# Seven-product block multiplication in the first batch, the factor sum and the gate rows on GpSimd: an AdaLN transformer block on one core

## The chip, the cores and the metric

The kernel runs on one core of a Trainium2 chip. The metric is the device time of one execution in microseconds, the median of several runs. The core has five engines that run side by side and meet through semaphores: TensorE (PE, matrix products into PSUM), VectorE (DVE), ScalarE (ACT), GpSimd (POOL) and SyncE (SP, which here only issues transfers). SP, ACT and POOL each have a queue of their own for DMAs. Each engine runs its instructions in the order that was fixed when the kernel was built. A waiting instruction holds up all that stand behind it.

## What is computed

Four batches of 1024 tokens with 512 channels, all in float32. Each batch is normalised, scaled and shifted by rows that come from a condition vector, goes through attention, is normalised again and goes through a sum of eight 512 x 512 factors.

```python
x = L0_attn_hidden_states                                   # (4, 1024, 512)
mod = (_silu(L0_c) @ L0_wmod).reshape(4, 6, 1, -1)
sa, ca, ga, sb, cb, gb = (mod[:, k] for k in range(6))
ga = (2 * (ga >= 0) - 1) * jnp.maximum(jnp.abs(ga), 0.25)   # gb alike
h = _layernorm(x) * (1 + ca) + sa
qf, kf = h @ Wq.T, h @ Wk.T                                 # rank 64, the same for all 16 heads
attn = softmax(qf @ kf.T)
x = x + ga * ((attn @ (h @ Wv.T)) @ Wo.T)
h = _layernorm(x) * (1 + cb) + sb
x = x + gb * (jnp.einsum('btd,rde->bte', h, factors) / math.sqrt(8) + bias)
```

All heads have the same scores, so one attention matrix per batch is enough, and Wv and Wo are folded into one 512 x 512 matrix (`wvo`). With n the normalised input, the kernel computes Z = attn @ n and then Z @ (scaled wvo). The shift `sa` gives one row per batch, `c1`, which is added to x.

## The kernel before

**One batch.** Tokens are kept as eight tiles of 128. `ln1` (L395) normalises a half of the batch (four tiles) with a reciprocal root on GpSimd (`rstd_of`, L343, the tiles `r_a` and `r_f`) and VectorE passes. The half is transposed: in batch 0 on TensorE, later by VectorE in blocks of 32 x 32 and sixteen 64 KB moves from SBUF to SBUF (`hT_by_dma` L428, `move_blocks` L416; staging tiles `st`, two buffers). `project` (L458) makes queries and keys, `scores` (L505) makes two token tiles of scores and their exponentials, and `transpose_probs` (L540) brings these into `PT`, again by sixteen moves on SP. `scale_wqk` (L450) scales the query and key weights for one batch.

**Z.** For each half of the queries Z is a product over 1024 keys. Batch 0 uses `z_steps` (L572): eight steps, each with four matmuls 512 columns wide, and a ScalarE copy out of PSUM after every second step. Batches 1 to 3 use `z_steps_by_seven` (L636). It cuts both operands in 2 x 2 quarters and needs seven products of quarters (m1 to m7, eight matmuls 256 wide each) where eight would be usual. The sums of quarters that this takes are made by `n_sums` (L612, four GpSimd passes over 128 x 1024, once per batch, three of them into staging tiles and one in place), by `p_sums` (L630, two VectorE passes per half, one of them into the tile `t`), by two more VectorE passes inside m1 and m5, and by adds of the products on VectorE and, in m7, GpSimd.

**Rows.** `shift_rows` (L298) adds up `c1`, `gates` (L308) makes the gate rows `ga`, `gb` and the gated bias on VectorE, four partitions high and 512 wide. `publish` writes a row to DRAM, and `spread` (L239) reads it back into all 128 partitions. The tile `rows` has the buffer in which later the scaled matrices `w` (`make_w`, L696) and `f` (`make_f`, L705) lie.

**The factor sum.** `sum_factors` (L325) runs on GpSimd after the first half of batch 0: sixteen loads of two 128 x 512 pieces into four staging buffers, and 28 adds of 128 x 512 into `fsum`.

**The second part.** `attn_out` (L716) multiplies Z by `w` and adds to x, `ln2` (L734) normalises and transposes by moves (into `st` tiles), `ffn` (L771) multiplies by `f` and stores. The FFN of a batch runs among the Z steps of the next batch's first half.

**Order.** The main loop (L819 to L902) is written out by hand: for each batch the steps of the first half with other work between them, then the steps of the second half with the projections and scores of the next batch between them (`todo`, at the `places`), then `n_sums`, `attn_out`, `ln2`. A scheduler orders each engine's instructions, close to program order; `tc.keep_in_program_order` pins an instruction. PSUM for products has four buffers (`ps_m`) and for scores two (`ps_s`).

Of the kernel before, what the change touches and what calls it, by code (L numbers as in the profile page):

```python
# [30 lines left out]
def kernel(  # L31
# [123 lines left out]
    rows = wbp.tile([32 + B, 4, D], F32, tag="w", name="rows")  # L155
    rows_a, rows_b = rows[0:B], rows[32 : 32 + B]
    biasb = rows_a[:, 3, :]
    nc.sync.dma_start(out=biasb, in_=bias.to_broadcast([B, D]))
    load_xa(1, 0)

# [61 lines left out]
    def gate(g, dst, name):  # L222

        sg = bcp.tile([32 + B, D], F32, tag="bc", name=f"gsign_{name}")[32 : 32 + B]
        ab = bcp.tile([32 + B, D], F32, tag="bc", name=f"gabs_{name}")[32 : 32 + B]
        nc.vector.tensor_scalar(sg, g, 0.0, 2.0, ALU.is_ge, ALU.mult)
        nc.vector.scalar_tensor_tensor(ab, g, -1.0, g, ALU.mult, ALU.max)
        nc.vector.tensor_scalar(ab, ab, 0.25, None, ALU.max)
        nc.vector.scalar_tensor_tensor(dst, sg, -1.0, ab, ALU.add, ALU.mult)
# [9 lines left out]
    def spread(name, b):  # L239
        tl = bcp.tile([P, D], F32, tag="bc", name=f"bc_{name}_{b}")  # L240

        queue = nc.gpsimd if name == "gb" or b == 0 else nc.sync
        queue.dma_start(out=tl, in_=rows_d[name][b : b + 1, :].to_broadcast([P, D]))
        return tl
# [53 lines left out]
    def shift_rows(ps):  # L298
        c1 = rows_a[:, 2, :]
        nc.scalar.copy(c1, ps[:B, :])  # L300
        for kc in range(1, KC):
            nc.vector.tensor_tensor(c1, ps[32 * kc : 32 * kc + B, :], c1, ALU.add)
# [5 lines left out]
    def gates():  # L308
        ga, gb, c1 = rows_a[:, 0, :], rows_a[:, 1, :], rows_a[:, 2, :]
        gate(rows_b[:, 0, :], ga, "ga")  # L310
        publish(ga, "ga")
        nc.vector.tensor_tensor(c1, c1, ga, ALU.mult)
        publish(c1, "c1")
        gate(rows_b[:, 3, :], gb, "gb")
        nc.vector.tensor_tensor(biasb, biasb, gb, ALU.mult)
        publish(biasb, "gbias")
        nc.vector.tensor_scalar(gb, gb, 1.0 / math.sqrt(NR), None, ALU.mult)
        publish(gb, "gb")

    fsum = const.tile([P, KC, D], F32, name="fsum")  # L320
# [4 lines left out]
    def sum_factors():  # L325
        for kc in range(KC):
            for r in range(0, NR, 2):
                f = stage(f"factor_{kc}_{r}").rearrange("p (r d) -> p r d", r=2)
                if kc == 0:

                    nc.scalar.copy(f[0:1, 0, 0:1], ZT[0, 0][0:1, 2, 0:1])
                nc.gpsimd.dma_start(
                    out=f, in_=factors[r : r + 2, ts(kc, P), :].rearrange("r p d -> p r d")
                )
                acc = fsum[:, kc, :]
                if r == 0:
                    nc.gpsimd.tensor_tensor(acc, f[:, 0], f[:, 1], ALU.add)
                else:
                    for k in range(2):
                        nc.gpsimd.tensor_tensor(acc, acc, f[:, k], ALU.add)  # L340
# [65 lines left out]
    bc_c1 = {}  # L406
# [21 lines left out]
    def hT_by_dma(b, g):  # L428
# [9 lines left out]
        move_blocks(st, hT.rearrange("p r k w -> p r (k w)"))  # L438
# [11 lines left out]
    def scale_wqk(b):  # L450
        w = qkp.tile([P, KC, 2 * R], F32, tag="wqkb", name=f"wqk_{b}")
        for kc in range(KC):
            nc.vector.tensor_scalar(
                w[:, kc, :], wqk[:, kc, :], first["ca1"][:, kc, b : b + 1], None, ALU.mult
            )
        wqkb[b] = w
# [83 lines left out]
    def transpose_probs(b, p):  # L540
# [6 lines left out]
            pt_tile(b, half)[:, pair].rearrange("p r j w -> p r (j w)"),  # L547
# [18 lines left out]
    def softmax(b, p):  # L566
        scores(b, p)
        transpose_probs(b, p)

    ZT = {}  # L570

    def z_steps(b, half):  # L572

        zt = ztp.tile([P, KC, GW], F32, tag="zt", name=f"zt_{b}_{half}")
        ZT[b, half] = zt
        hold, steps = {}, []

        def part(dc, jh):
            if jh == 0:
                hold[dc] = psum_mm(f"ps_z_{b}_{half}_{dc}")  # L580
            for j in halves(jh):
                nc.tensor.matmul(  # L582
                    hold[dc], xn1[b, jh][:, j - jh * GT, ts(dc, P)], PT[b, half][:, :, :, j, :],
                    start=(j == 0), stop=(j == NT - 1),
                )
            if jh == 1:
                dst, src = zt[:, dc, :], hold[dc]
                if by_dma(b, half):

                    dst = dst.rearrange("p (h t r a) -> p h r t a", h=2, t=2, r=NQ)  # L590
                    src = src.rearrange("p (h r t a) -> p h r t a", h=2, t=2, r=NQ)
                nc.scalar.copy(dst, src)

        for dc in range(KC):
            for jh in range(2):
                steps.append(lambda dc=dc, jh=jh: part(dc, jh))
        return steps
# [14 lines left out]
    def n_sums(b):  # L612
# [7 lines left out]
        tt(s1, a21, a22, ALU.add)  # L620
# [15 lines left out]
    def z_steps_by_seven(b, half):  # L636
# [8 lines left out]
        def product(k, a, m):  # L645
            ps = psum_mm(f"ps_z_{b}_{half}_m{k}")
            for dc in range(2):
                for j in range(GT):

                    nc.tensor.matmul(  # L650
                        ps[:, ts(dc, 2 * P)], a[:, j, ts(dc, P)],
                        m[:, :, j].rearrange("p r (k a) -> p k r a", k=2),
# [287 lines left out]
```

## Time and profile before

| what | value |
|---|---|
| runs | 541.03, 540.96, 538.78 us; median 540.96 |
| the profiled execution | 538.85 us |
| its span | 537.0 us, granted clock 0.996 |
| TensorE / VectorE / ScalarE / GpSimd busy in the span | 523.4 / 362.1 / 93.2 / 158.5 us |
| first step of Z, batch 0 | 56.84 us |
| first product of Z, batch 1 | 161.29 us |
| GpSimd: factor sum with the sums for batch 1, first to last pass | 87.96 to 145.6 us |
| `fsum` add, 128 x 512, GpSimd | 1.27 us each |
| `n_sums` pass, 128 x 1024, GpSimd | 2.35 us each, 3.38 for two of the first ones |
| `p_sums` pass, 128 x 1024, VectorE | 1.22 us each |
| a 512 KB factor load, issue to landing | 3.7 / 5.1 / 10.2 us (least, median, most) |
| a 64 KB block move on SP, issue to landing | 2.0 us median |

The page counts an engine as busy from the start to the end of its instructions; matmuls overlap, so that the distance between the starts of two groups says better what a group costs. Lines of the timeline give start, length, engine, line of the kernel, operation, output and inputs, shapes and count; what stands in brackets behind them is the idle time before the instruction and what ended it. Lines of the chain give start, length, engine, tile, line.

### The profile page before, as it was taken

What the parts mean: (1) busy time and instruction counts of PE and PEld (TensorE: products, weight loads), DVE (VectorE), ACT (ScalarE), POOL (GpSimd) and SP (SyncE); (2) the same over time, 40 slices, a digit from 0 to 9 for tenths busy, and PEclk for the clock granted to TensorE, in tenths of its full rate; (3) what the DMA queues carried; (4) which work ended last, traced back from release to release, by engine and by line L of the source; (5) the groups of instructions that cost most, each with busy time, mean ns of one, the idle gap of its engine ahead of it and who ended that gap; (6) DMA issues with size and microseconds to landing.
All of it is one profiled execution on the core that took longest, in us unless ns stands there. A gap on an engine that the chain in (4) does not pass through costs nothing.

```text
span 537.0 us, 5254 instructions
## 1 busy us (share of the span) xinstructions
PE 523.4 (97%) x1688; PEld 290.9 (54%) x1688; DVE 362.1 (67%) x580; ACT 93.2 (17%) x155; POOL 158.5 (30%) x177
## 2 busy tenths in 40 slices
PE   6999899999999999999999999999999999999997
PEld 3533344433448457766448457765448457855444
DVE  4629987264899974359999965358999315577761
ACT  1327500122302020123102010123202200000110
POOL 1002136999801353323001343323001134021010
PEclk9989999999999999999999999999999999999999
DMA  8942369858444667404444656404444415001142
GB/s 319 380 182 68 89 179 262 247 165 244 109 118 113 174 209 226 134 1 97 118 113 113 183 157 209 110 0 99 122 119 107 142 59 214 21 0 32 47 157 78
DMA packets 39570, 74.07 MB, mean 138 GB/s; under 512 B 9988, under 2 KB 10756, under 8 KB 39544
## 3 DMA queue, kind: packets, MB, share of 16 engines
q1 hardware_dynamic: 27368, 41.06, 26.8%
q0 software_dynamic: 8624, 28.48, 17.0%
q10 hardware_dynamic: 3552, 4.21, 2.9%
q8 instruction: 13, 0.21, 0.2%
q14 instruction: 13, 0.11, 0.1%
HBM read 35.93 MB, written 8.42 MB: 83 GB/s over the span
## 4 chain that ended last, share of the span: by engine, by line
PE 58%; DVE 20%; issue 8%; SPq 5%; DMA 4%; POOL 3%; ACT 2%; DVEq 0%; POOLq 0%; ACTq 0%
PE ps_z_m L650 17%; PE ps_f L779 15%; PE ps_z L582 8%; PE ps_qk L469 5%; PE ps_o L720 5%; SPq L426 5%; PE ps_wvo L186 3%; DVE pr L544 3%; DVE nm L531 2%; DMA pt<-pr 2%; PE ps_sc L515 2%; ACT pr L535 2%; DVE hT_f L365 2%; DVE x L725 1%; DVE bn_a L356 1%
## 5 line engine op out<-in xcount | busy, mean ns | idle before, releaser
L779 PE MATMUL ps_f<-f,hT_f 128*128 128x512 f32 (+1 forms) x264 | 111.8, 580 | 0.8 <-ACT hT_f L765 0.5
L720 PE MATMUL ps_o<-w,zt 128*128 128x512 f32 x256 | 111.8, 594 | 0.5 <-DVE zt L688 0.5
L779 PEld LDWEIGHTS ps_f<-f,hT_f 128*128 128x128 f32 x264 | 49.9, 190 | 59.4 <-issue 54.3
L720 PEld LDWEIGHTS ps_o<-w,zt 128*128 128x128 f32 x256 | 48.3, 190 | 61.2 <-issue 56.4
L650 PE MATMUL ps_z_m<-pt,xn_a 128*128 128x256 f32 x288 | 65.3, 380 | 0.0
L650 PEld LDWEIGHTS ps_z_m<-pt,xn_a 128*128 128x128 f32 x288 | 54.6, 190 | 11.4 <-issue 2.4
L582 PE MATMUL ps_z<-pt,xn_a 128*128 128x512 f32 x128 | 56.9, 597 | 0.0
L784 DVE TENSOR_TENSOR x<-ps_f,x 128x512 f32<-128x512 f32 (+1 forms) x33 | 21.9, 670 | 43.8 <-PE ps_f L779 43.8
L535 ACT ACTIVATE pr<-ps_sc,nm 128x1024 f32<-128x1024 f32 x32 | 35.5, 1111 | 79.1 <-DVE nm L531 40.9
L650 PE MATMUL ps_z_m<-pt,s 128*128 128x256 f32 x192 | 43.6, 380 | 0.0
L650 PEld LDWEIGHTS ps_z_m<-pt,s 128*128 128x128 f32 x192 | 36.3, 190 | 8.5 <-issue 3.9
L582 PEld LDWEIGHTS ps_z<-pt,xn_a 128*128 128x128 f32 x128 | 23.8, 190 | 31.6 <-issue 30.8
L515 PE MATMUL ps_sc<-kT,qT 64*128 64x512 f32 x128 | 38.2, 626 | 2.3 <-ACT pr L535 2.3
L531 DVE TENSOR_REDUCE nm<-ps_sc 128x1 f32<-128x1024 f32 x32 | 37.6, 1210 | 2.4 <-PE ps_sc L515 2.4
L765 ACT ACTIVATE hT_f<-st_f,mod_sb,mod_cb 128x512 f32<-128x512 f32 x28 | 20.6, 803 | 96.6 <-DVE bn_f L356 40.2
L351 POOL TENSOR_TENSOR r_f<-v_f,mhalf 128x4 f32<-128x4 f32 x8 | 9.3, 1165 | 94.8 <-DVE v_f L347 94.8
L725 DVE SCALAR_TENSOR_TENSOR x<-ps_o,ri,x 128x512 f32<-128x512 f32 x32 | 23.8, 743 | 15.1 <-PE ps_o L720 15.0
L544 DVE STREAM_TRANSPOSE pr<-pr 128x2048 f32<-128x2048 f32 x14 | 32.2, 2299 | 0.9 <-DMA pt<-pr 0.7
L351 POOL TENSOR_TENSOR r_a<-v_a,mhalf 128x4 f32<-128x4 f32 x8 | 9.2, 1152 | 78.8 <-DVE v_a L347 78.6
L340 POOL TENSOR_TENSOR fsum<-fsum,factor 128x512 f32<-128x512 f32 x24 | 30.4, 1273 | 0.4
L469 PE MATMUL ps_qk<-hT_a,wqk 128*128 128x512 f32 x64 | 30.5, 624 | 0.0
L483 DVE TENSOR_SCALAR qT<-ps_qk,qbias 64x512 f32<-64x512 f32 x8 | 5.9, 743 | 36.1 <-PE ps_qk L469 36.1
(124 smaller groups left out, 582.7 us busy)
## 6 DMA issues: line engine op xcount, KB each, us to landing
pt<-pr SPq DMA_DIRECT2D x224, 64.0 KB, 2.0
factor<-in_factors_dram POOLq DMA_DIRECT2D x16, 512.0 KB, 5.1
hT_a<-st_a SPq DMA_DIRECT2D x96, 64.0 KB, 4.9
out_dram<-x POOLq DMA_DIRECT2D x24, 256.0 KB, 2.6
x<-in_x_dram POOLq DMA_DIRECT2D x24, 256.0 KB, 5.3
xa<-in_x_dram POOLq DMA_DIRECT2D x20, 256.0 KB, 4.0
st_f<-hT_f SPq DMA_DIRECT2D x62, 64.0 KB, 2.0
st_f<-hT_f ACTq DMA_DIRECT2D x60, 64.0 KB, 2.1
```

The source lines that it names most:

```text
L340: nc.gpsimd.tensor_tensor(acc, acc, f[:, k], ALU.add)
L426: queues[i % len(queues)].dma_start(out=dst[ts(c, Q), r], in_=src[ts(r, Q), c])
L469: nc.tensor.matmul(ps[: 2 * R, :], wqkb[b][:, kc, :], hT[:, kc] if b == 0 else hT[:, :, kc], start=(kc == 0), stop=(kc == KC - 1),)
L515: nc.tensor.matmul(ps[:, ts(h, 512)], qT[h * R : (h + 1) * R, ts(i, P)], kT[h * R : (h + 1) * R, :], start=True, stop=True,)
L531: nc.vector.tensor_reduce(nm, ps, AX.X, ALU.max, negate=True)
L535: nc.scalar.activation(pr, ps, AF.Exp, bias=nm, scale=1.0, accum_out=den[:, k : k + 1])
L544: nc.vector.transpose(pr2, pr2)
L582: nc.tensor.matmul(hold[dc], xn1[b, jh][:, j - jh * GT, ts(dc, P)], PT[b, half][:, :, :, j, :], start=(j == 0), stop=(j == NT - 1),)
L650: nc.tensor.matmul(ps[:, ts(dc, 2 * P)], a[:, j, ts(dc, P)], m[:, :, j].rearrange("p r (k a) -> p k r a", k=2), start=(j == 0), stop=(j == ...
L720: nc.tensor.matmul(ps, ZT[b, half][:, kc, ts(j, P)], wb[b][:, kc, :], start=(kc == 0), stop=(kc == KC - 1),)
L725: nc.vector.scalar_tensor_tensor(xi, ps, rinv[b][:, t : t + 1], xi, ALU.mult, ALU.add)
L779: nc.tensor.matmul(ps, hT2[b, g][:, kc, ts(j, P)], fb[b][:, kc, cols], start=(kc == 0), stop=(kc == KC - 1),)
```

## The change

Four things are changed.

1. Batch 0 uses the seven products too, for both halves; the old `z_steps` is gone and `z_steps_by_seven` takes its name. So `n_sums(0)` and `p_sums(0, ·)` come in, and in batch 0 the two adds of m7 go to VectorE. Places for the next batch's projections and scores in batch 0's second half are steps 1 to 5 instead of 0 and 2 to 5.
2. The factors are summed in passes of 128 x 1024, into `fsum`, which is loaded with factor 0 by SP at the start. Factors 1 to 7 come as 1 MB loads on GpSimd's queue into the two `st` buffers of the block moves. A one-element copy that reads `w_0` stands before the first add, and `sum_factors()` moves into the second half of batch 0, with `n_sums(1)` behind it.
3. The gate rows, the sum of `c1` and the gated bias are made on GpSimd, with scratch rows in spare partitions of the tile `rows`. `gates` is split in `attention_rows` and `ffn_rows`; the first comes earlier, the second later. ScalarE copies three instead of one of the four pieces of `c1`.
4. In batch 0 half of the moves of the last probabilities and of the second half's transposes go to ACT's queue. `add_c1(0)` moves into the second half, and the query and key weights of batches 2 and 3 are scaled at a fixed place.

```diff
-    rows = wbp.tile([32 + B, 4, D], F32, tag="w", name="rows")
+    rows = wbp.tile([64 + B, 4, D], F32, tag="w", name="rows")
+    fsum = const.tile([P, KC, D], F32, name="fsum")
+    nc.sync.dma_start(out=fsum, in_=factors[0].rearrange("(kc p) d -> p kc d", p=P))
...
+    def gate(g, parts, dst):
+        half, size = parts
+        tensor_scalar = nc.gpsimd.tensor_scalar
+        tc.keep_in_program_order(
+            tensor_scalar(half, g, 0.0, 0.5, ALU.is_ge, ALU.subtract)
+        )
+        tensor_scalar(size, g, 1.0, None, ALU.mult)
+        nc.gpsimd.tensor_tensor(size, size, half, ALU.mult)
+        tensor_scalar(size, size, 0.125, 4.0, ALU.max, ALU.mult)
+        nc.gpsimd.tensor_tensor(dst, size, half, ALU.mult)
...
     def shift_rows(ps):
+        for kc in range(KC - 1):
+            nc.scalar.copy(rows_a[:, kc, :], ps[32 * kc : 32 * kc + B, :])
         c1 = rows_a[:, 2, :]
+        nc.vector.tensor_tensor(c1, ps[32 * (KC - 1) : 32 * (KC - 1) + B, :], c1, ALU.add)
...
+    def attention_rows():
+        ga, c1 = rows_a[:, 0, :], rows_a[:, 2, :]
+        for kc in range(2):
+            nc.gpsimd.tensor_tensor(c1, c1, rows_a[:, kc, :], ALU.add)
+        gate(rows_b[:, 0, :], [rows_c[:, k, :] for k in range(2)], ga)
+        publish(ga, "ga")
+        nc.gpsimd.tensor_tensor(c1, c1, ga, ALU.mult)
+        publish(c1, "c1")
+    def ffn_rows():
+        gb = rows_a[:, 1, :]
+        gate(rows_b[:, 3, :], [rows_c[:, k, :] for k in range(2, 4)], gb)
+        nc.gpsimd.tensor_tensor(biasb, biasb, gb, ALU.mult)
+        publish(biasb, "gbias")
+        nc.gpsimd.tensor_scalar(gb, gb, 1.0 / math.sqrt(NR), None, ALU.mult)
+        publish(gb, "gb")
...
     def sum_factors():
+        f = {}
+        def load(r):
+            f[r] = stp.tile([P, KC, D], F32, tag="st", name=f"factor_{r}")
+            nc.gpsimd.dma_start(
+                out=f[r], in_=factors[r].rearrange("(kc p) d -> p kc d", p=P)
+            )
+        load(1)
+        load(2)
+        late = small.tile([P, 1], F32, tag="late", bufs=1, name="late")
+        nc.gpsimd.tensor_copy(late[0:1], wb[0][0:1, KC - 1, 0:1])
+        for r in range(1, NR):
+            for k in range(2):
+                part = fsum[:, ts(k, 2), :]
+                add = nc.gpsimd.tensor_tensor(part, part, f[r][:, ts(k, 2), :], ALU.add)
+                tc.keep_in_program_order(add)
+            if r + 2 < NR:
+                load(r + 2)
...
     def n_sums(b):
+        if b == 0:
+            nc.gpsimd.tensor_copy(s1[0:1, 0, 0:1], wqkb[0][0:1, KC - 1, 0:1])
...
+            engine = nc.vector if b == 0 else nc.gpsimd
+            engine.tensor_tensor(c(0, 1), c(0, 1), c(1, 1), ALU.add)
+            engine.tensor_tensor(c(1, 1), c(1, 1), c(1, 0), ALU.add)
...
     scale_wqk(0)
+    n_sums(0)
...
+    p_sums(0, 0)
...
         if b == 0:
+            both = nc.sync, nc.scalar
             z0 = z_steps(b, 0)
             z0[0]()
-            softmax(0, 3)
+            softmax(0, 3, *both)
+            z0[1]()
+            shift_rows(ps_c1)
+            attention_rows()
+            z0[2]()
             ln1(1, 0)
             hTn = [hT_by_dma(1, 0)]
-            shift_rows(ps_c1)
-            for step in z0[1:3]:
+            for step in z0[3:5]:
                 step()
             ln1(1, 1)
-            hTn.append(hT_by_dma(1, 1))
-            gates()
-            scale_wqk(nb)
-            for step in z0[3:5]:
-                step()
-            add_c1(0, range(NT))
+            bc_ga[0], bc_c1[0] = spread("ga", 0), spread("c1", 0)
+            hTn.append(hT_by_dma(1, 1, *both))
             for step in z0[5:]:
                 step()
+            scale_wqk(nb)
             second_channels()
-            sum_factors()
+            ffn_rows()
...
-            places = (0, 2, 3, 4, 5)
+            places = (1 if b == 0 else 0, 2, 3, 4, 5)
...
+            if b == 0 and k == 0:
+                add_c1(b, range(NT))
             if k == 1:
                 make_w(b)
+                if b == 0:
+                    sum_factors()
+                    n_sums(1)
...
         if nb is not None:
-            n_sums(nb)
+            if b > 0:
+                n_sums(nb)
```

## The prediction

> **What bounds the kernel now.** I read the busy table first, then TensorE's timeline, then the chain that ended last, in order of time, and last GpSimd's and VectorE's timelines where the first batch hands over to the second (85 to 185 us).
>
> ```profile
> PE 523.4 (97%) x1688; PEld 290.9 (54%) x1688; DVE 362.1 (67%) x580; ACT 93.2 (17%) x155; POOL 158.5 (30%) x177
> ```
>
> TensorE is nearly always busy, so fewer products should pay, unless something else then ends last. TensorE's timeline gives the prices (start, length, count):
>
> ```profile
> 87.19 7.13 PE L582 MATMUL ps_z<-pt,xn_a 128*128 128x512 f32 x16
> 142.10 1.99 PE L515 MATMUL ps_sc<-kT,qT 64*128 64x512 f32 x8
> 161.29 3.62 PE L650 MATMUL ps_z_m<-pt,xn_a 128*128 128x256 f32 x16
> 164.74 3.62 PE L650 MATMUL ps_z_m<-t,s 128*128 128x256 f32 x16
> ```
>
> From start to start a quarter of an eight-product half costs 6.97 us (94.16 - 87.19) and one of seven products 3.45 us (164.74 - 161.29). The chain in order of time shows what TensorE meets next:
>
> ```profile
> 153.59 1.05 POOL r_f L351
> 154.66 1.92 DVE hT_f L365 x4
> 157.24 2.22 DVE hT_f L755
> ...
> 180.29 1.32 DVE xn_a L365 x3
> 182.26 7.13 PE ps_f L779 x16
> ```
>
> From 143 to 182 us the chain is hardly on TensorE: VectorE works without a pause, and TensorE's third FFN tile (182.26) waits 0.5 us for VectorE to free PSUM. VectorE's list starts after the GpSimd reciprocal root r_f, 27.6 us before (182.26 - 154.66). So a lead that TensorE wins in batch 0 reaches the end only as far as r_f moves. GpSimd ahead of it:
>
> ```profile
> 142.03 2.34 POOL L623 TENSOR_TENSOR s<-xn_a,s 128x1024 f32<-128x1024 f32 x1
> 144.34 1.25 POOL L340 TENSOR_TENSOR fsum<-fsum,factor 128x512 f32<-128x512 f32 x1
> 145.55 0.57 POOL L243 DMA_DIRECT2D bc_gb<-rows_gb  x1
> 153.59 1.04 POOL L351 TENSOR_TENSOR r_f<-v_f,mhalf 128x4 f32<-128x4 f32 x1 [7.48 <-DVE v_f L347]
> ```
>
> GpSimd had 7.5 us to spare. The last view is the contention (groups of instructions, and VectorE's timeline):
>
> ```profile
> L700 DVE SCALAR_TENSOR_TENSOR w<-wvo,mod_ch_a,bc_ga x16: 741/746/2061, 89.0 to 448.5; 128x512 f32<-128x512 f32 x16
> 88.97 7.33 DVE L700 SCALAR_TENSOR_TENSOR w<-wvo,mod_ch_a,bc_ga 128x512 f32<-128x512 f32 x4
> 207.23 2.73 DVE L700 SCALAR_TENSOR_TENSOR w<-wvo,mod_ch_a,bc_ga 128x512 f32<-128x512 f32 x4
> ```
>
> The same four passes take 2.73 us alone and 7.33 us beside GpSimd's sums: each waits for a whole GpSimd instruction. It goes the other way too: GpSimd's s took 3.38 us at 223.92, where a VectorE pass over two SBUF tiles was running, against 2.35 us alone.
>
> **The change, part by part.** *Products.* Sixteen quarter-steps in pairs (eight of 6.97) become 14 products of 3.45: 55.8 - 48.4 = 7.4 us less on TensorE. In the built order the first two score tiles of batch 1 are no longer split by a projection: 4 matmuls took 1.9 us each time (104.56, 112.67), 8 take 1.99 at 142.10; 1.9 us less. TensorE's lead is about 9 us.
>
> *VectorE in batch 0.* Per half it gains four 1024-wide passes (1.2 us, L633, L634, L662, L667), five PSUM adds of 0.69 and two SBUF adds of 0.6, some 9.5 us; it loses the gates (11 passes, 6.5 us) and two row sums (1.4). Its idle time covers that: 5.1 us before 83.98, 11.7 before 110.20, 6.8 before 135.34. Without the cover, an add that frees PSUM would stall the product after next; I allow 0.6 us at m4.
>
> *GpSimd before the products.* The four sums of batch 0 (4 x 2.35) run at 28 to 38 us, where GpSimd waited 30 us for v_a; the key weights of batch 1 (0.86 us at 36.6) may wait for one of them, before 2.4 us of idle. The gate rows run from about 61 to 72 us, in its 13.7 us of idle before 65.5; behind them stand the second root r_a of batch 1 (ready to start at 73), four xa loads and two spreads. Two-input rows I cost as the 512-wide sum, 1.27 us. One-input rows no row shows: between 0.29 (the 128-wide select) and 1.27; I take 0.8, near the nearer width. The FFN rows (some 7 us) end at 86.
>
> A page only: the Trainium skill, GPSIMD Engine Reference, section Engine selection, keeps elementwise work on VectorE and calls GpSimd about half as fast with two inputs and about line rate with one. By that the one-input rows would be 0.5 us, and the rows 1 to 2 us shorter, ahead of a wait anyway.
>
> *Queues.* SP loses 16 of 64 moves (0.65 us each) to ACT, and gets the first factor's 1 MB load, long landed when SP starts moving at 55.4. ACT waits in its queue for the last transposes (about 79.4), ends its moves at 84.7, and its next work, the copy of m1, comes at 87.5. SP is done at about 88 instead of 100.6. The batch 2 and 3 weights are scaled earlier, in VectorE's 1.5 us idle at 199.75.
>
> *The factor sum.* It now starts when w_0 is written. When is that? m1 starts at 56.84 like the old product; 3.45, score halves 1.91, six products 20.7, the allowance 0.6 and transposes 0.6 give the second half at 84.1. Two products and a projection (6.9 + 3.4) reach 94.5; VectorE then has the tail of the t update, qT 0.7 and w 2.73: 98.4. No allowance and no t tail: 97.5; every two-input pass of the first half behind one GpSimd row: 101. GpSimd's queue from there, all in front of r_f:
>
> - 14 sums of 1024 x 2.35 = 32.9 and the four sums of batch 1, 9.4
> - six factor loads issued, at 0.54 for 128 rows of 2 KB (x) and 0.72 for 256 (factor), so an estimated 1.08 for 512: 6.5
> - two spreads 1.1 and a one-element copy 0.1
>
> Together 50.0 us: 148.4 if nothing waits. Then VectorE's two-input passes while it runs (2 x 0.6 for m7, 2 x 1.2 for the p sums): 0 to 3.6 us; I take 3.0, since s took the whole of such a wait. Then landings: a load is wanted 1.08 + 4.7 + 1.08 = 6.9 us after its issue. Two 512 KB loads issued 1.95 us apart (116.67, 118.62) were in after 7.2 us; 1 MB of wmod took 8.5 among other loads. So waits are 0 to 4 us over five loads; I take 1.0. GpSimd is free at 152.4.
>
> The Trainium skill sees a danger there: SBUF — State Buffer, section SBUF: two separate sides, says a VectorE pass in a two-port mode keeps GpSimd from writing the descriptors of its own DMAs. The factor issues here took 704 to 736 ns, the one at 113.50 beside such a pass included, so the row shows none of it; by the page each of the few meetings would add the length of one such pass, 0.27 us (wqk).
>
> *VectorE up to r_f.* Scores 6 and 7 of batch 1, at 142.10 before, come at about 133; v_f was ready 11.4 us later, now up to 3.6 more for the two p sums under GpSimd's lock: 148. So GpSimd, not VectorE, ends last, and r_f starts at 152.4 against 153.59. VectorE's order from there to 182 is the same, and it is full, so everything after moves by **-1.2 us**; later batches are unchanged. Sum: 538.85 (the profiled execution: span 537.0 and 1.85 around it) - 1.2 = 537.7. The three runs (541.03, 540.96, 538.78) average 540.26, 1.4 above the profiled one: **539.1 us**. The cost hidden here is TensorE's lead: it stands idle for about 8 us between 165 and 175.
>
> **Rivals.** *A, the forecast, no change:* GpSimd is free between 150.9 and 156.3, -2.7 to +2.7 us. For it: the work listed is 50 us whatever its order. *B, faster:* sums meet no passes and loads land in time; GpSimd is free at 148.4, r_f waits for v_f at 148 instead, -5.1 us: 535.2. Against it: the 3.38 us of s. Its far end, that VectorE catches up between 155 and 182 and TensorE keeps all 9 us, gives 531; against it, no idle in that list but three waits of 0.9 us on GpSimd. *C, slower:* the factor chain takes the place of TensorE. With w_0 at 101, 50.0 of work, 3.6 of passes and 4 of landings GpSimd is free at 158.6, +5.0: 545.3. It decides from 156.3 on. For it: two buffers where four were, and all of it in front of r_f in one queue. *D, that the products stay eight,* is excluded by the built order (14 groups of eight 256-wide matmuls).
>
> **How the numbers follow.** A measurement of this kernel can't tell less than 0.5%, 2.7 us, from no change (its runs differ by 2.2). A has 0.43, B 0.33 (0.04 of it the far end), C 0.24; these are the chances of same, faster, slower. A alone spans 536.4 to 541.8. The range reaches to B's and C's ends: 535.0 to 545.0.
>
> **What would show it.** Right: products at 3.45 us apart in batch 0; the first of batch 1 near 152 instead of 161.3; GpSimd without a gap from w_0 to r_f; VectorE idle before hT_f for GpSimd; TensorE idle before ps_f. r_f ready well before v_f would be B; long waits of fsum for factor loads, or w_0 after 101, C. Wrong altogether: a stall of TensorE before 130 us (a late t or PSUM), or a late r_a, neither of which I find.

## The result and the profile after

| | before | after |
|---|---|---|
| median of 20 runs each | 540.64 us (538.78 to 541.95) | 542.08 us (540.34 to 544.54) |
| after / before | | 1.0029, interval 1.0017 to 1.0042 |
| profiled execution, span | 538.85 us, 537.0 us | 542.55 us, 540.8 us |
| GpSimd's root r_f starts | 153.59 us | 156.09 us |
| TensorE's first product of batch 1 | 161.29 us | 158.11 us |
| TensorE's first qk of batch 2 | 216.78 us | 220.78 us |

The kernel became 1.4 us slower, 0.29%: less than the 0.5% named as the bound of "no change", but on the other side of zero from the forecast. The profiled execution of before lies 1.8 us below its median, that of after 0.5 us above, so the two traces differ by more (3.8 us of span) than the medians do. The busy table of after:

```profile
PE 518.0 (96%) x1784; PEld 310.5 (57%) x1784; DVE 376.4 (70%) x589; ACT 91.5 (17%) x149; POOL 188.6 (35%) x175
```

TensorE has 5.4 us less to do (523.4 before) and yet the span grew: work was removed from a place that no longer ends last. TensorE's timeline (start, length, engine, line, operation, tiles, count, and in brackets the idle time ahead and who ended it), first in batch 0, then in batch 1:

```profile
66.85 3.62 PE L657 MATMUL ps_z_m<-pt,xn_a 128*128 128x256 f32 x16
70.30 3.62 PE L657 MATMUL ps_z_m<-pt,s 128*128 128x256 f32 x16
...
158.11 3.62 PE L657 MATMUL ps_z_m<-pt,xn_a 128*128 128x256 f32 x16
...
165.01 3.62 PE L657 MATMUL ps_z_m<-pt,xn_a 128*128 128x256 f32 x16
173.62 6.05 PE L657 MATMUL ps_z_m<-pt,s 128*128 128x256 f32 x16 [4.99 <-DVE pt L668]
179.50 13.90 PE L790 MATMUL ps_f<-f,hT_f 128*128 128x512 f32 x32
```

Products in batch 0 stand 3.45 us apart (70.30 - 66.85), as forecast, and TensorE comes to batch 1 3.2 us earlier than before. Then it stands still for 4.99 us before product m6, and the 16 matmuls of m6 take 6.05 us instead of 3.62. The chain of waits in order of time says what m6 waited for:

```profile
156.09 1.06 POOL r_f L373
157.18 1.92 DVE hT_f L387 x4
...
172.34 1.15 DVE pt L668
173.62 6.05 PE ps_z_m L657 x16
```

From r_f to m6 it is VectorE's list again, as before; and r_f itself starts 2.5 us later than before (153.59). GpSimd's timeline shows why (L347 issues the load of a factor):

```profile
75.89 1.07 POOL L373 TENSOR_TENSOR r_a<-v_a,mhalf 128x4 f32<-128x4 f32 x1
...
95.31 0.81 POOL L347 DMA_DIRECT2D factor<-in_factors_dram  x1 [0.62 <-DMA hT_a<-st_a]
...
103.58 0.76 POOL L347 DMA_DIRECT2D factor<-in_factors_dram  x1 [5.04 <-DMA hT_a<-st_a]
...
104.49 4.65 POOL L359 TENSOR_TENSOR fsum<-fsum,factor 128x1024 f32<-128x1024 f32 x2
...
153.65 2.35 POOL L627 TENSOR_TENSOR s<-xn_a,s 128x1024 f32<-128x1024 f32 x1
156.09 1.05 POOL L373 TENSOR_TENSOR r_f<-v_f,mhalf 128x4 f32<-128x4 f32 x1
```

There is no gap ahead of r_f: GpSimd is what ends last. Its sum starts at 104.49, not at the forecast 98.4, and the instruction just ahead of it, the issue of factor 2's load at 103.58, had waited 5.04 us for the moves out of the st buffer that it takes over. VectorE's timeline shows the other thing that the sum waits for, w_0:

```profile
77.00 1.92 DVE L387 TENSOR_SCALAR xn_a<-xa,mv,r_a 128x512 f32<-128x512 f32 x4 [5.37 <-DMA pt<-pr]
...
92.38 5.32 DVE L434 TENSOR_TENSOR x<-x,bc_c 128x512 f32<-128x512 f32 x8
...
99.41 2.73 DVE L708 SCALAR_TENSOR_TENSOR w<-wvo,mod_ch_a,bc_ga 128x512 f32<-128x512 f32 x4
```

VectorE normalizes batch 1's tile at 77.00, right after r_a, which takes 1.07 us from 75.89 on (the bracket names a DMA; the same row in the run p2 below names r_a). From there to the end of w_0 (102.14 = 99.41 + 2.73) no row of VectorE shows idle time. So w_0 was late because VectorE was, and the sum was later still by 2.35 us because of the buffer.

### The profile page after: what moved, and what is told of

Read it like the earlier page. It is cut to its first block, busy times and chain, and to the rows that moved or that the text cites. A ratio compares the mean times of both kernels' runs of the same rounds, so it can differ in the third digit from the quotient of the medians.

```text
span 540.8 us, 5461 instructions
## 1 busy us (share of the span) xinstructions
PE 518.0 (96%) x1784; PEld 310.5 (57%) x1784; DVE 376.4 (70%) x589; ACT 91.5 (17%) x149; POOL 188.6 (35%) x175
## 4 chain that ended last, share of the span: by engine, by line
PE 51%; DVE 22%; issue 9%; DMA 7%; SPq 6%; POOL 2%; ACT 1%; ACTq 1%; DVEq 0%; POOLq 0%
PE ps_z_m L657 18%; PE ps_f L790 17%; SPq L448 6%; PE ps_o L731 5%; PE ps_qk L494 5%; DVE nm L556 3%; PE ps_wvo L188 3%; DMA pt<-pr 3%; DVE pr L569 3%; DMA hT_a<-st_a 2%; DVE hT_f L387 2%; DVE bn_f L378 1%; DVE x L736 1%; ACT pr L560 1%; PE ps_sc L540 1%
## 5 line engine op out<-in xcount | busy, mean ns | idle before, releaser
L657 PE MATMUL ps_z_m<-pt,xn_a 128*128 128x256 f32 x384 | 87.3, 381 | 0.6 <-DVE zt L690 0.6
L657 PEld LDWEIGHTS ps_z_m<-pt,xn_a 128*128 128x128 f32 x384 | 72.6, 190 | 16.3 <-issue 2.6
L657 PE MATMUL ps_z_m<-pt,s 128*128 128x256 f32 x256 | 60.6, 392 | 5.0 <-DVE pt L668 5.0
L657 PEld LDWEIGHTS ps_z_m<-pt,s 128*128 128x128 f32 x256 | 50.0, 197 | 17.2 <-issue 10.5
L540 PE MATMUL ps_sc<-kT,qT 64*128 64x512 f32 x128 | 36.1, 624 | 2.5 <-ACT pr L560 2.5
L666 ACT COPY zt<-ps_z_m 128x512 f32<-128x512 f32 x8 | 4.7, 585 | 176.2 <-PE ps_z_m L657 104.4
L359 POOL TENSOR_TENSOR fsum<-fsum,factor 128x1024 f32<-128x1024 f32 x14 | 32.9, 2368 | 1.8 <-DMA factor<-in_factors_dram 1.6
L798 POOL DMA_DIRECT2D out_dram<-x x24 | 13.2, 549 | 57.8 <-DVE x L795 47.5
L657 PE MATMUL ps_z_m<-t,xn_a 128*128 128x256 f32 x128 | 29.4, 383 | 0.5 <-DVE zt L678 0.5
L657 PE MATMUL ps_z_m<-t,s 128*128 128x256 f32 x128 | 29.0, 380 | 0.0
```

The costliest lines, as they stand in the source:

```text
L359: add = nc.gpsimd.tensor_tensor(part, part, f[r][:, ts(k, 2), :], ALU.add)
L540: nc.tensor.matmul(ps[:, ts(h, 512)], qT[h * R : (h + 1) * R, ts(i, P)], kT[h * R : (h + 1) * R, :], start=True, stop=True,)
L657: nc.tensor.matmul(ps[:, ts(dc, 2 * P)], a[:, j, ts(dc, P)], q, start=(j == 0), stop=(j == GT - 1),)
```

## The experiments

The theory after the result: *the end of the kernel follows r_f, and r_f follows the start of the factor sum*. Rivals: the landings of the factor loads, the SP queue, the halved rate of m6's matmuls, and the products themselves. In the expectations W stands for "VectorE, held up behind r_a, makes w_0 late", H for "TensorE's clock falls in its idle time". Ratios are to before, measured on the same chip beside each kernel, with 95% intervals, and need not equal the quotient of the two medians; after stands at 1.0029. One profiled execution of each was read, and the times of one kernel spread by 2 to 9 us, so a single r_f is good to a us or two, not to tenths.

**Half of the factors (e3).** Does r_f follow the sum at all? Factors 4 to 7 are left out, so the FFN weights lack them.

```diff
-        for r in range(1, NR):
+        for r in range(1, NR // 2):
...
-            if r + 2 < NR:
+            if r + 2 < NR // 2:
```

> Factors 4 to 7 are left out of the sum (the FFN's weights then lack them), so GpSimd has 21 us less ahead of r_f. Theory G (GpSimd's queue sets r_f): r_f starts when v_f is written, and v_f, free of GpSimd's lock, comes at about 151.5 instead of 155.9; -4.5 us at r_f, no idle of TensorE worth naming ahead of the fourth product, no halved clock there, which takes off another 1.4: -5.5 to -6 us (536.5). Rival V (VectorE's added passes in batch 0 and 1 bind): v_f stays at 153.8 or later, -2 us or less.

Measured: 535.45 us (534.4 to 539.4), ratio 0.9907 [0.9884, 0.9930]. GpSimd's and TensorE's timelines:

```profile
150.50 1.05 POOL L373 TENSOR_TENSOR r_f<-v_f,mhalf 128x4 f32<-128x4 f32 x1 [19.20 <-DVE v_f L369]
```

```profile
168.57 3.62 PE L657 MATMUL ps_z_m<-pt,s 128*128 128x256 f32 x16
```

GpSimd now has 19.20 us to spare and r_f waits for VectorE's v_f, 3.1 us earlier than before; m6 has neither the idle time nor the slow matmuls. Removing half of the sum is worth 6.6 us against after (542.08 - 535.45). The chain in front of r_f is what the change lost its gain to.

**One load on another queue (e2).** Factor 2's load, whose wait kept GpSimd from the first add, is put on SP.

```diff
-            nc.gpsimd.dma_start(
+            (nc.sync if r == 2 else nc.gpsimd).dma_start(
```

> The load of factor 2 is issued by SP instead of GpSimd, so that GpSimd doesn't stand behind the buffer that the block moves still read. Theory Q: the sum starts at the landing of factor 1 or at w_0, about 102.7 instead of 104.5, r_f -1.7 us; TensorE idles about 3.3 us ahead of the fourth product of batch 1 instead of 5.0, about as long as the 3.4 us after which the clock fell in the changed kernel: -1.7 us if it still falls, -3.1 if it doesn't. Rival R: the 5 us wait only takes the place of waits for factors that would have come later: within 0.5 us.

Measured: 541.39 us (539.9 to 546.8), ratio 1.0030 [0.9997, 1.0063]. In the trace the sum starts 1.7 us earlier (102.77), right after w_0, and r_f 1.3 us earlier (154.79). In the time that can't be told from after. The 2.35 us of the buffer are real, but they are the smaller part; w_0 is the larger. The clock fell here as well: TensorE stood idle for 4.93 us ahead of m6, whose matmuls took 5.30 us.

**Rows of the gate earlier (e5).** If W holds, GpSimd's order ahead of r_a sets w_0. The first four rows of the attention gate are issued as soon as their input exists; only the last stays where it was, just ahead of the row's way to DRAM.

```diff
-        nc.gpsimd.tensor_tensor(dst, size, half, ALU.mult)
+        return lambda: nc.gpsimd.tensor_tensor(dst, size, half, ALU.mult)
...
-        gate(rows_b[:, 0, :], [rows_c[:, k, :] for k in range(2)], ga)
+        ga_last()
...
+    ga_last = gate(rows_b[:, 0, :], [rows_c[:, k, :] for k in range(2)], rows_a[:, 0, :])
```

> The first gate's rows, all but the last pass, are put on GpSimd as soon as the modulation rows are there (about 54 us), ahead of the shift rows; nothing else is moved. GpSimd was idle from 54.8 to 61.5. Theory W (w_0 hangs on r_a): VectorE runs without a pause from the normalization that waits for r_a (77.0) to the end of w_0 (102.1), and r_a stands behind the rows (75.9, where v_a was ready at 71.6). Then r_a comes at 71.7 to 72.7, w_0 3 to 4 us earlier (98 to 99), the factor sum starts at 100 to 101, r_f moves by -3 to -4 us, time -3 to -4 (-5 if TensorE's idle falls under 3.4 us and its clock holds). Rival P (TensorE's products and their waits set w_0, as the forecast had it): w_0 stays at 101 or later, less than 1 us. Rival K: the rows at 54 to 61 hold up VectorE's two-input passes there by 2 us or more, v_a comes later, and the gain is lost.

Measured: 540.49 us (539.2 to 544.7), ratio 1.0002 [0.9982, 1.0022]. r_a comes 3.8 us earlier (72.09) and w_0 3.1 us earlier (99.06), so W is right. But the st buffer comes free only 1.9 us earlier than in after, and the sum starts at 102.62; GpSimd's timeline:

```profile
101.71 0.76 POOL L347 DMA_DIRECT2D factor<-in_factors_dram  x1 [6.28 <-DMA hT_a<-st_a]
```

So two conditions were late side by side, and curing one leaves the other. In the profiled execution, which took 544.67 us, GpSimd also waited 2.08 and 3.47 us for factor loads.

**Both cures (e8)**, the edits of e5 and e2 together.

> The same early gate rows, and the load of factor 2 issued by SP. Theory W with Q: besides, the sum starts at w_0 or at the landing of factor 1 (98 to 99 us) instead of at the freeing of the buffer; r_f -4.5 to -5.5 us against the changed kernel (151 to 151.5), TensorE's idle ahead of the fourth product 3 us or less, clock not halved: time -5.5 to -7 (535.5 to 536.5). Rival: factor 2's landing only takes over, no more than the early gate alone.

Measured: 542.78 us (537.2 to 546.6), ratio 1.0016 [0.9987, 1.0045], without the longest run. A miss: the sum starts at 100.24, 4.2 us earlier than in after, and GpSimd is done at 150.0, but r_f still starts at 156.15, now waiting 6.12 us for v_f. VectorE's timeline shows a new cost:

```profile
117.53 5.48 DVE L686 TENSOR_TENSOR zt<-zt 128x512 f32<-128x512 f32 x1
...
124.07 4.68 DVE L687 TENSOR_TENSOR zt<-zt 128x512 f32<-128x512 f32 x1
...
130.96 0.65 DVE L690 TENSOR_TENSOR zt<-ps_z_m,zt 128x512 f32<-128x512 f32 x1
```

These two adds, both of whose operands lie in SBUF, now meet the factor sums and take seven to eight times what the add of the same width with a PSUM operand takes (0.65). The prediction had priced them at 0.6 us under VectorE's idle time. A sum that starts earlier can fall on them; in e5 and p2 the second add took 4.48 and 4.36 us, in after the first one 2.13.

**Eight products in batch 0 again (e9)**, with everything else of the change kept; batch 0's part sums go with them.

```diff
-    n_sums(0)
...
-            z0 = z_steps(b, 0)
+            z0 = z_eight(b, 0)
...
-        z1 = z_steps(b, 1)
+        z1 = z_steps(b, 1) if b > 0 else z_eight(b, 1)
```

> Batch 0 with eight products per half as before the change (and without its sums on GpSimd and VectorE); the factor sum, the rows on GpSimd and the queues as in the changed kernel. Theory G: TensorE's shorter batch 0 buys nothing, since r_f waits for GpSimd. TensorE works 7.4 us longer and VectorE some 19 us less before 135 us; w_0 is written at 96 to 99, the sum starts at the freeing of the second half's buffer (101 to 103) instead of 104.5, r_f -1.5 to -3 us; TensorE has no idle time of 3 us ahead of the fourth product of batch 1, and its clock holds there: -3 to -4.5 us against the changed kernel (537.5 to 539). Rival L: the seven products do win their 3 us of lead at the end, and without them the time is 545 or more.

Measured: 545.86 us (544.6 to 547.4), ratio 1.0096 [1.0071, 1.0122]. I had expected it faster; it is slower. VectorE's qT now waits 6.74 us for TensorE's projection, w_0 ends at 104.7 and r_f starts at 156.87. So the seven products do pay: beside the rest of the change they are worth 0.67% (1.0096 - 1.0029), some 3.6 us. The two traces show 2.0 us of it (542.8 - 540.8), 0.8 at r_f, which two earlier conditions, the buffer (104.85) and w_0, hold together here; the rest I can't place. Part of it may be chance: in this execution the granted clock was at 0.50 from 57.8 to 61.2, and the first eight matmuls of Z took 5.40 instead of 3.70 us; in after it was at 0.50 for as long near 30 us. The other parts of the change, without the products, cost about 1% (1.0096).

**TensorE kept busy (e6).** Ten products of 512 columns more, into the PSUM tile that m6 then overwrites, fill the idle time before m6. (The view counts each float32 product twice, ten as x20.)

```diff
+            if (b, half, k) == (1, 0, 6):
+                for _ in range(10):
+                    nc.tensor.matmul(
+                        ps, xn1[1, 1][:, 0, ts(0, P)], xn1[1, 1][:, 1, :], start=True, stop=True
+                    )
```

> Ten extra products of 128x512, whose result is overwritten, fill most of TensorE's 5 us wait ahead of the fourth product of batch 1. Theory H: the clock halves because TensorE stood idle; with the extra products those 16 matmuls take 3.6 us instead of 6.05, and the time falls by up to 1.4 us (VectorE then frees the third FFN tile's place only at r_f + 27.6); the planner also orders a few VectorE passes after them differently, +-1 us. Rival: the clock falls for another reason (what the chip does at that time): the 16 matmuls take 6 us still, time unchanged or later.

Measured: 552.42 us, ratio 1.0213 [1.0173, 1.0252]. TensorE's timeline:

```profile
168.03 8.75 PE L653 MATMUL ps_z_m<-xn_a 128*128 128x512 f32 x20
176.61 3.62 PE L662 MATMUL ps_z_m<-pt,s 128*128 128x256 f32 x16
...
192.92 9.18 PE L795 MATMUL ps_f<-f,hT_f 128*128 128x512 f32 x16 [5.82 <-DVE zt L683]
```

With no idle time ahead, m6's 16 matmuls take 3.62 us: H is right about the 6.05. The time is of no use: the planner, given longer work on TensorE, put transposes ahead of VectorE's zt adds, TensorE then waited 5.82 us, and the 16 matmuls behind that took 9.18 us instead of 7.03. H is seen a second time there.

**Two sums behind the root (e7).** Instead of starting the chain earlier, it is made shorter: the last two part sums of batch 1 go behind r_f.

```diff
-        tt(s2, s1, a11, ALU.subtract)
-        tt(s4, a12, s2, ALU.subtract)
+        def rest():
+            tc.keep_in_program_order(tt(s2, s1, a11, ALU.subtract))
+            tt(s4, a12, s2, ALU.subtract)
+        if b == 1:
+            later.append(rest)
+        else:
+            rest()
...
+            if b == 0:
+                later.pop()()
```

> The last two of the four sums of batch 1 (4.7 us of GpSimd) are put behind r_f instead of ahead of it; the planner then also puts VectorE's two sums of probabilities (t, pt) behind r_f. Theory G: r_f starts when GpSimd is free, near 151.3, or at v_f: -4 to -5 us at r_f; the two sums and VectorE's passes after r_f hold each other up, 1 to 3 us; time -2 to -4. Rival V: VectorE's list from r_f to the third FFN tile only gets longer by what was put into it (t and pt, 2.4 us, and the locks, 3 us): time unchanged or later.

Measured: 537.93 us (535.9 to 541.2), ratio 0.9944 [0.9917, 0.9971]. r_f starts at 151.18, 4.9 us earlier than in after, and waits for v_f; m6's idle time is 0.90 us and its matmuls run at the full rate. The moved sums now lie beside hT_f, whose four passes take 5.97 us instead of 1.92, and the kernel is still 0.56% faster than before. This one edit turns the change from a loss into a gain.

**With the early gate (e11: e5 and e7)**

> The early gate rows and the last two sums of batch 1 behind r_f together. Theory: GpSimd is ready for r_f at 149.5 to 150, but v_f comes at 150.5 to 151, so r_f moves by no more than 0.7 against the two sums alone (537.9): 537.2 to 538. Rival: the earlier sum meets the block moves and VectorE's passes, v_f comes later, 539 or more.

Measured: 537.60 us (535.2 to 539.5), ratio 0.9942 [0.9918, 0.9966]; **and with the load on SP too (e10: e5, e2 and e7)**

> The same with the load of factor 2 on SP. Theory V: GpSimd is ready for r_f at 147 to 148, v_f sets it at 150.5 to 151 or later: VectorE's two adds over zt alone are held up by GpSimd's pairs of sums in some runs (5.5 and 4.7 us in the run of the early gate with this load). 537 where they are not, 540 to 541 where they are: a wide spread. Rival G: every us that GpSimd gains still counts, 535.5.

Measured: 538.53 us (533.9 to 541.0), ratio 0.9954 [0.9925, 0.9982]. Neither differs from e7 beyond its interval: once r_f waits for v_f, an earlier start of GpSimd shows no further gain in the times. (In the one execution of e11 that was traced, its second fastest, r_f does come 3.4 us earlier than in e7's, 147.78, and more than the expected 0.7.)

**The zt adds off VectorE (b5)**: e10, and the adds that e8 showed waiting are given to GpSimd, as in the later batches, for all but the first half of batch 0.

```diff
-            engine = nc.vector if b == 0 else nc.gpsimd
+            engine = nc.vector if (b, half) == (0, 0) else nc.gpsimd
```

> The same, and the two adds over zt after the fifth product of batch 0's second half are put on GpSimd (2.5 us there), as in the later batches, so that VectorE meets no lock there. Theory V: v_f at 150 to 150.5 in all runs, GpSimd ready for r_f at 150: 536 to 537, with less spread than the kernel before it. Rival: GpSimd's queue is longer again and r_f comes at 151.5 or later: 538 or more.

Measured: 536.17 us (535.5 to 537.7), ratio 0.9920 [0.9901, 0.9938], 0.8% faster than before and 1.1% faster than after. Against e10 the spread falls from 7.0 to 2.2 us; the intervals of the two overlap. GpSimd's and TensorE's timelines:

```profile
148.70 1.05 POOL L373 TENSOR_TENSOR r_f<-v_f,mhalf 128x4 f32<-128x4 f32 x1 [1.27 <-DVE v_f L369]
```

```profile
168.59 3.69 PE L662 MATMUL ps_z_m<-pt,s 128*128 128x256 f32 x16 [0.90 <-DVE pt L673]
```

r_f starts 7.4 us earlier than in after (156.09 - 148.70), GpSimd is 1.27 us ahead of VectorE there, and m6 starts 5.0 us earlier, at full rate. The two engines end nearly together there, so that shifting more work from GpSimd to behind r_f should have little left to give; that was not tried.

**The SP queue.** In after SP issues its moves of hT_a from 75.57 on over 22.49 us, and 10.2 us of that is one wait (78.7 to 89.0) for an earlier hT_a move. It must be one of ScalarE's, which were issued from 81.94 on, since no move took over 6.0 us to land. e1 puts all moves of batch 1 back on SP:

```diff
-            hTn.append(hT_by_dma(1, 1, *both))
+            hTn.append(hT_by_dma(1, 1))
```

> All 16 moves of batch 1's second half are issued by SP, as before the change; the 8 of the last transposes of batch 0 stay on ScalarE. Theory Q (queues): SP's 10.2 us pause after its fifth move of the first half comes from lanes that ScalarE's moves of the second half hold. It goes; the two waits of ps_qk (1.0 and 1.7 us) and most of the 5.0 us wait of the second factor load go; the factor sum starts at w_0, near 102 instead of 104.3; r_f moves 156.1 to about 154.0. TensorE's lead grows by up to 2.7, so it idles 5 us or more ahead of the fourth product of batch 1 and its clock still halves there: time about -2 us against the changed kernel (540). Rival R (rows): the gate rows on GpSimd are what is late, SP's pause is covered: within 0.5 us. Rival L: TensorE's lead carries to the end: -4.8 us.

Measured: 548.09 us (547.2 to 549.4), ratio 1.0137 [1.0098, 1.0177], the opposite of what was expected. SP has no pause any more and is done at 95.8 instead of 98.1. But the planner dealt the two st buffers out otherwise: factor 2 got the one that factor 1 holds, its load went out at 107.8 only, behind factor 1's adds, and GpSimd waited 5.88 us for it; r_f starts at 161.75. **e12** gives that load to SP as well (e1 and e2):

> All moves of batch 1's second half on SP alone, and the load of factor 2 issued by SP behind them, so that it can't slip behind the first sums on GpSimd as it did when the moves alone were put on SP (548.1 us). Theory: that kernel was slow because factor 2 was then loaded late (GpSimd waited 5.9 us for it) and the sum met the block moves later on; with the load in place the sum starts at w_0 near 102.4, r_f comes at 154 to 155, and the time is that of the load alone (541.4), 540 to 542: the pause of SP itself costs nothing at the end. Rival: the moves of the second half on SP alone are what costs, or the order that the planner then gives to scores and sums: 546 to 548 again.

Measured: 547.53 us, ratio 1.0114 [1.0084, 1.0144], a miss again, for the same reason. GpSimd's timeline:

```profile
115.27 2.36 POOL L359 TENSOR_TENSOR fsum<-fsum,factor 128x1024 f32<-128x1024 f32 x1 [6.75 <-DMA factor<-in_factors_dram]
```

In **p2** the two buffers get names of their own, so that factor 2 can't be given factor 1's:

```diff
-    stp = ctx.enter_context(tc.tile_pool(name="stp", bufs=2))
+    stp = ctx.enter_context(tc.tile_pool(name="stp", bufs=1))
...
-            f[r] = stp.tile([P, KC, D], F32, tag="st", name=f"factor_{r}")
+            f[r] = stp.tile([P, KC, D], F32, tag=f"st{1 - r % 2}", name=f"factor_{r}")
```

> All moves of batch 1's second half on SP, the load of factor 2 on SP behind them, and the two buffers told apart by name, so that factor 2 gets the second half's buffer and not that of factor 1 (which cost 6.8 us of waiting in the kernel before this one). Theory: SP has no pause, factor 2 is loaded by 97 to 98 us and in by 104; the sum starts at w_0 near 102.5 and meets no wait for factor 2; r_f at 154 to 155 as with the load alone on SP, time 540 to 542. Then the shared lanes cost nothing beyond the late buffer. Rival: moves on SP alone are themselves worse, 546 or more. Second rival: freed of the pause, the projections no longer wait (2.4 us), r_f comes at 152 and the time is 538 or less.

Measured: 540.89 us (539.2 to 544.8), ratio 1.0001 [0.9982, 1.0019]. The load goes out at 96.64, nothing waits for it, the sum starts right after w_0 (102.14) and r_f at 154.48: as e2. So e12 lost its 6 us to the shared buffer, and e1, with the same wait, most likely too; SP's pause of 10.2 us cost nothing that shows beyond the late buffer. **p3** is b5 with SP alone and these buffers:

> The fastest kernel so far (536.2: early gate, load of factor 2 on SP, two sums behind r_f, two zt adds on GpSimd) with the second half's moves on SP alone and the buffers told apart by name. Theory: its r_f waits for v_f, and v_f for the block moves of the probabilities, not for the second half: 535.5 to 537. Rival: the projections' waits (0.4 and 2.3 us there) reach the end: 533.5 to 534.5. Rival: the moves on SP alone cost, 540 or more.

Measured: 536.42 us, ratio 0.9921 [0.9903, 0.9940], the same as b5, with r_f at 148.69. Which queue moves the blocks doesn't matter for the end here.

The same relation runs through all of them (spans and starts of r_f in us):

| kernel | r_f | span | span - r_f |
|---|---|---|---|
| e11 | 147.8 | 533.4 | 385.6 |
| p3 | 148.7 | 534.6 | 385.9 |
| b5 | 148.7 | 534.3 | 385.6 |
| e3 | 150.5 | 533.8 | 383.3 |
| e10 | 150.5 | 536.0 | 385.5 |
| e7 | 151.2 | 536.8 | 385.6 |
| before | 153.6 | 537.0 | 383.4 |
| p2 | 154.5 | 540.2 | 385.7 |
| e2 | 154.8 | 538.7 | 383.9 |
| after | 156.1 | 540.8 | 384.7 |
| e8 | 156.2 | 539.5 | 383.3 |
| e9 | 156.9 | 542.8 | 385.9 |
| e5 | 157.9 | 542.9 | 385.0 |
| e12 | 160.8 | 545.4 | 384.6 |
| e1 | 161.8 | 545.4 | 383.6 |

Over 14 us of r_f the rest stays between 383.3 and 385.9. What differs has a pattern: the kernels with two sums behind r_f (e7, e10, e11, b5, p3) lie at 385.5 to 385.9, those where TensorE runs at half clock for 6.8 us around m6 (after, e5, e9, p2) at 384.7 to 385.9, the others at 383.3 to 384.6. Only e6, with its other order on VectorE, falls out (393.4).

## Why the prediction was wrong

**What held.** The mechanism: r_f carries the time, GpSimd has no gap ahead of it, VectorE stands idle 1.08 us before hT_f for GpSimd, TensorE before ps_f. Rival A, that the list is about 50 us whatever its order, is nearly right too: the forecast for the stretch from the first sum to r_f was 54.0 us (50.0, 3.0 and 1.0), measured 51.6 (156.09 - 104.49). Within it the issues took 0.76 instead of 1.08, landings 0.91 and 0.68, each factor sum 2.33, and meeting VectorE's passes cost the sums of batch 1 some 1.9 instead of 3.0. Part of the difference is only where the line is drawn: the forecast counted one load and one spread behind the start (1.6 us) that in the run lie ahead of the first sum.

**The step that failed** is the start of the factor sum: "VectorE then has the tail of the t update, qT 0.7 and w 2.73: 98.4". Measured: 104.49, 6.1 us later. Three things are in it.

- w_0 was worked out along TensorE alone. VectorE was taken to be free when the projection was done; it had been full since 77.00, when r_a let it go on, and the list left out the 5.32 us of the eight passes that add the constant to x. w_0 ended at 102.14, 3.7 us late. The text had a bound of 101 for it, for another reason, and took 98.4. TensorE's projection was late too (it ended at 98.03, not 94.5), but that did not set w_0: in p2 it ended at 96.62, and w_0 moved only 0.2 us, as r_a did. e5 shows the cause: r_a 3.8 us earlier gives w_0 3.1 us earlier.
- r_a itself came late for two reasons. A row with one input takes 1.5 (one operation) to 1.95 us (two), not the 0.8 chosen: the range was bounded from above by the 1.27 of a two-input pass, as if one input could not cost more. It does: 1.94 against 1.27, next to each other. Of the attention gate's three such rows two stand in this stretch; one ran earlier, at 53.30 or before, so that the net loss is 1.5 us. And the first of the two adds for `c1` took 3.30 instead of 1.26 us:

```profile
61.50 4.64 POOL L323 TENSOR_TENSOR rows<-rows 4x512 f32<-4x512 f32 x2 [6.71 <-DVE rows L313]
```

  From 61.34 to 63.68 VectorE made two passes over SBUF for the seven products of batch 0. In e9, which has no such passes there, both adds took 1.25. That is 2 us for which the forecast had no term. The attention rows ran from 61.5 to 75.9 instead of to 72, the FFN rows 13.3 us instead of 7.
- The load of factor 2 stands on GpSimd's queue ahead of the first add and needs the st buffer of the second half's moves. No term was there for that wait: 2.35 us, as e2 and p2 show.

The start was 6.1 us off, the stretch after it 2.4 us the other way, which is luck: r_f came 3.7 us later than forecast (156.09 against 152.4), 2.5 us later than before.

**The term that was missing.** "The cost hidden here is TensorE's lead: it stands idle" gave the idle time no price. Its clock fell during it. The windows of 0.2 us show it (start and end, length, busy time of TensorE, its weight loads, VectorE, ScalarE and GpSimd with counts, the granted clock, DMA share, GB/s):

```profile
171.20:171.40 0.20, 0.00 (x0) 0.00 (x0) 0.20 (x2) 0.00 (x0) 0.00 (x0) 1.00 0.67 195
171.60:171.80 0.20, 0.00 (x0) 0.00 (x0) 0.20 (x2) 0.00 (x0) 0.00 (x0) 0.50 0.86 266
178.00:178.20 0.20, 0.20 (x2) 0.18 (x1) 0.20 (x2) 0.00 (x0) 0.00 (x0) 0.50 0.00 0
178.40:178.60 0.20, 0.20 (x2) 0.17 (x1) 0.20 (x2) 0.00 (x0) 0.00 (x0) 1.00 0.46 113
```

The granted clock is at one half from 171.6, 3.0 us after the last matmul ended (168.63), to 178.4, 4.8 us after m6 began. m6 loses 2.4 us (6.05 - 3.62); about 1.45 us of that lies beyond the point that VectorE's list allows, an estimate from when VectorE frees the next PSUM tile. With the 2.5 us of r_f that makes 4.0, which is the shift of the first qk of batch 2 (220.78 - 216.78), and the span's 3.8. By the traces, then, the forecast's -1.2 us missed by 3.7 at r_f and 1.4 to 1.5 at the clock. By the medians, of which the traces are one draw each, the loss is 1.4 us, 2.6 above the forecast; how that splits over the two isn't known. The lower clock is no chance of the one trace: its mean was 0.987 to 0.994 in all 20 executions of after, and 0.993 to 1.0 in those of before that ran beside the experiments.

**The lead of TensorE** was put at 9 us and came to 3.2. The products and score tiles gave 8.1 us; m1 started 0.9 us later than in before, and five waits of 0.5 to 1.7 us ahead of batch 1's products (5.15 us, 1.17 in before) took the rest, two of them (0.98 and 1.68) for hT_a. In p2, where SP has no pause, neither of these two is there. It cost nothing: the lead was idle time later anyway.

**The rivals.** C described what happened, a factor chain in front of r_f that takes the place of TensorE, but not its size: with w_0 at 101 it needed 3.6 us of passes and 4 of landings on top, and got 1.9 us of passes and 1.6 of landings. B's condition, r_f waiting for v_f, came true only when the chain was shortened or started earlier (e3, e7 and the kernels built on it, e8; by 0.4 us in e2 and p2). The statement that only a late r_a or a stall before 130 us would make the forecast wrong altogether, "neither of which I find", was itself the miss: r_a came at 75.89, not 73.

**Still open.** How far the runs' spread (up to 9 us in e8, 3 in before) comes from the landings of the factor loads was read from single traces only and not tried by itself. b5's four parts were not each taken away in turn.

## What to carry to other kernels

When work is moved to an engine that has time to spare, write down every condition that the first moved instruction waits for (the data, the buffer, each instruction queued ahead of it) and follow each of them back through its own engine; here the sum's start was traced on one engine, and two others set it. Before work is made cheaper, find what the lead runs into: TensorE's 3 us ended as idle time in front of an unmoved root, and moving two sums behind that root was worth more than everything that started them earlier. Give idle time of TensorE a price.

## What the runs showed of the hardware

*The clock.* From 50 us to the end of the matmuls all idle times of TensorE of 2.61 us and more (up to 6.57) came with a granted clock of 0.50, and 16 matmuls of 256 columns then mostly took 5.1 to 6.5 us instead of 3.62; none of 1.86 us or less did. Between them it went both ways. For the same matmuls of qk 1.91 (e7) and 2.21 us (e5) halved the clock, 2.00 (e6), 2.14 (e10) and 2.25 (b5) did not. A wait of 2.03 to 2.15 us near 55 us, in all runs but before, halved it in four of fifteen (e6, e8, e9, e11). In e7 and e5 the clock fell 0.4 and 0.9 us after work had begun again, and the half clock lasted about 3.4 us (e5: 102.2 to 105.6), in after 6.8 us (171.6 to 178.4), twice that. So an idle time of over 2 us can cost 1.5 to 2.8 us on top of itself. Idle time is not all: near 30 us the clock was at 0.50 for 3.4 us in eight of the sixteen traces, before and after among them, with no idle time over 0.3 us just ahead, but with matmuls of only 8 and 4 columns (25.22 to 27.37 in after).

The Trainium skill, TensorE: Matmul & The Clock Gate, Part 1, describes half speed after an idle window of about 3.4 us and full speed after a busy one, with windows that run freely. The stretches of 3.4 and 6.8 us, and the chance between 1.9 and 2.3 us, agree with such windows. The runs also halved the clock after idle times well below the 3.4 us that the page names, and there the measurement decides.

*The shared port.* Some of VectorE's passes over SBUF wait for whole GpSimd instructions, small ones too: v_f, 128x4, took 2.17 us instead of 0.15 under the last part sum, hT_f's four passes 5.97 instead of 1.92 (e7), zt's add 5.48 instead of 0.68 (e8). The adds with a PSUM operand took 0.65 to 0.69 everywhere, and the transposes of hT_f from SBUF to SBUF 2.28 to 2.31. It goes the other way too, as the 3.30 us of `c1`'s first add show.

The Trainium skill, SBUF — State Buffer, section Who interferes with whom, says that the pair of ports is locked for a whole instruction by whoever comes first, for VectorE passes with two SBUF inputs or in a two-port mode. The rows agree; 5.48 us is more than the 2.33 of one sum, so such a pass can lose to two in a row.

*GpSimd's rows.* At 4x512 a pass with one input takes longer than one with two: 1.50 us (one operation) and 1.94 (two) against 1.27.
